# A gated cross-attention and mixture-of-experts kernel: the last pair of token tiles routed in another order

## The chip, the cores and the metric

The kernel runs on one NeuronCore of a Trainium2 chip. The core has five engines that run their own instruction streams and wait for one another through semaphores: TensorE (PE, matmuls; PEld is its weight load), VectorE (DVE), ScalarE (ACT), GpSimd (POOL) and SyncE (SP). Data moves between the chip's main memory and the on-chip memory through DMA queues, which SyncE, ScalarE and GpSimd issue to. The metric is the device time in microseconds (us) of one execution. A profile is one recorded execution; its times count from the span's start.

## The reference

The inputs are x (8 batches of 256 tokens, width 512), a context of 256 rows of 512 for each batch with a mask, two gates, a router (8 experts) and the experts' weights (512 to 192 and back). What is computed:

```
x = x + tanh(g_xattn) * attention(layernorm(x), ctx, ctx, mask)       # softmax over the unmasked rows, scale 1/sqrt(512)
xt = layernorm(x)                                                     # 2048 tokens
probs = softmax(xt @ w_router.T);  top_v, top_i = top_k(probs, 2);  top_v = top_v / sum(top_v)
for each token, over its two experts e:
    out += top_v * (silu(xt @ w_gate[e].T) * (xt @ w_up[e].T)) @ w_down[e].T
x = x + tanh(g_ffn) * out
```

Everything is float32. Which rows are masked and which experts a token takes depend on the data.

## The kernel before, in words

The 2048 tokens are 16 tiles of 128 tokens (NT = 16), in 8 pairs k of two tiles. There are two stages, and both are written out by hand in the order in which each engine is to take its work (`manual_schedule`).

**The routing stage** runs over steps s = 0 to 19 (line 579). Tile s gets its attention scores (`a_scores`), tile s - 1 its probabilities, its values and its router logits (`a_probs`, `a_values`), and tile s - 2 the centring of its updated row (`f_centre`) and a sum of squares (`f_square`). `a_values` (376) takes the two largest logits of each token (`max`, `max_index`, lines 386 and 387) and then adds the attention to x (line 388, the token update). Per pair, some steps later:

- `f_mark` (420): a one-hot mark of the expert of each choice, 128 x 32.
- `f_rank` (428): matmuls with a triangular matrix add the marks of this pair to a running count (`rank`), which gives each token its place in its expert's list; the place is split into a tile (`high`) and a row (`low`). `at_row` (line 441, VectorE) and `at_col` (line 445, four comparisons of 128 x 128 on GpSimd) are one-hot forms of the two.
- `f_table` (448): four matmuls of these add the token numbers to `table`, the list of tokens by place.
- `f_count` (455): two more matmuls bring the count up to date.
- `f_scale` (402): the variance and the difference of the two best logits on VectorE (lines 404, 406), then a power of -0.5 on GpSimd (407).
- `f_weigh` (410): weights from these on ScalarE (414 to 417), and the store of the pair's 256 rows, each with its scalars, to `xc_d` in main memory (418), issued from ScalarE.

After the last marks, `numbers` (509) works out on VectorE how many tiles each expert's list fills and where they begin: `u`, `nti`, `end`, `begin`, then `sel` (528), which selects the 46 expert tiles (23 for the first choices, 23 for the second), and `past`, `pn`, `eqi`, `nt_i` (530 to 535), the expert of each tile and the number of tiles. `read_table` (537) copies the table (539), and two matmuls with `sel` and one VectorE operation give `ids` (543), the token numbers of every expert tile. `last_constants` (493) makes constants that `numbers` reads (`ltile`, `keep`, `rowe`, `qplace`), on GpSimd, at step 15.

In the steps around the change the order of the last pair (k = 7) is: step 16: update of tile 15, `f_scale(6)`, `f_mark(7)`, `f_table(6)`; step 17: `f_rank(7)`, `f_square(15)`, `f_weigh(6)`, `f_count(7)`, `numbers`; step 18: `f_scale(7)`, `f_table(7)`, `read_table`; step 19: `f_weigh(7)`. Every engine takes its part of this in this order[...].

**The expert stage** (`run`, 700) takes 19 expert tiles of the first choices and 19 of the second. For each, GpSimd gathers 128 rows of `xc_d` by `ids` (line 640, up to four tiles ahead, and seven gathers before the first result is scattered). TensorE transposes them (181), applies the expert's gate and up weights (`gate_up`, 658) and its down weights (`down`, 682); GpSimd scatters the result (645), for the second choices after adding the first ones' result. The first gather needs `ids` and all eight row stores to have landed. The expert weights were loaded during the routing stage.

Of the kernel before, what the change touches and what calls it, by code (L numbers as in the profile page):

```python
# [9 lines left out]
FP = mybir.dt.float32  # L10
# [3 lines left out]
ALU = mybir.AluOpType  # L14
# [5 lines left out]
P = 128  # L20
# [26 lines left out]
def gated_xattn_moe(ctx: ExitStack, tc: tile.TileContext, x, xT, ctxn, ctxT, mask, maskT, g_x, g_f, wr, wgu, wd, out):  # L47
# [23 lines left out]
    def row(shape, name):  # L71
        return make(wk, 512, "row", 7, shape, name)
# [303 lines left out]
    def a_values(i):  # L376
        p, k, t = i // TT // 2, i // 2, i % 2
        if t == 0:
            KEEP["xr", k] = xrs[k % 4]
        lg = KEEP["xr", k][:, t, LG:LG + E1]  # L380
        prT, r, pcw = KEEP.pop(("prT", i)), KEEP.pop(("r", i)), KEEP.pop(("ppt", i))[:, P:2 * P]
        nc.tensor.matmul(pcw, lhsT=prT, rhs=cws[p], start=True, stop=True, skip_group_check=True)
        pav = bank([P, D], f"pav_{i}")
        nc.tensor.matmul(pav, lhsT=prT, rhs=cns[p], start=True, stop=True)  # L384
        nc.vector.scalar_tensor_tensor(lg, pcw[:, 0:E1], r, KEEP.pop(("xw", i)), ALU.mult, ALU.add)
        nc.vector.max(mx[:, i, :], lg[:, 0:E])
        nc.vector.max_index(ix[:, i, :], mx[:, i, :], lg[:, 0:E])
        nc.vector.scalar_tensor_tensor(xs[i], pav, r, xs[i], ALU.mult, ALU.add)

    def f_centre(i):  # L390
# [29 lines left out]
    def f_mark(k):  # L420
        m = marks[k % 2][:, NL:3 * NL]
        nc.vector.tensor_tensor(m.rearrange("p (t k e) -> p t k e", t=2, k=2), ecol.unsqueeze(1).broadcast_to([P, 2, 2, E]),
                                ix[:, 2 * k:2 * k + 2, 0:2].unsqueeze(3).broadcast_to([P, 2, 2, E]), ALU.is_equal)
# [4 lines left out]
    def f_rank(k):  # L428
        more(k, below, NL)
        more(k, ones, 0)  # L430
        at = sm_.tile([P, 2 * NL], FP, tag="at", bufs=2, name=f"at_{k}")
        nc.vector.tensor_mul(at, marks[k % 2][:, NL:3 * NL], rank[:, 0:2 * NL])
        pos = sm_.tile([P, 4], I32, tag="pos", bufs=2, name=f"pos_{k}")
        with nc.allow_low_precision(reason="whole numbers under 2 ** 16"):
            nc.vector.tensor_reduce(pos, at.rearrange("p (n e) -> p n e", n=4), AX.X, ALU.add)
        high = sm_.tile([P, 4], I32, tag="high", bufs=2, name=f"high_{k}")
        nc.vector.tensor_scalar(high, pos, 7, None, ALU.arith_shift_right)
        low = sm_.tile([P, 4], FP, tag="low", bufs=2, name=f"low_{k}")
        nc.vector.scalar_tensor_tensor(low, high, -float(P), pos, ALU.mult, ALU.add)  # L439
        at_row, at_col = row([P, 4, P], f"ar_{k}"), row([P, 4, P], f"ac_{k}")  # L440
        nc.vector.tensor_tensor(at_row, cols.unsqueeze(1).broadcast_to([P, 4, P]), high.unsqueeze(2).broadcast_to([P, 4, P]),
                                ALU.is_equal)
        for n in range(4):
            i = 2 * k + n // 2
            nc.gpsimd.tensor_scalar(at_col[:, n, :], cols, low[:, n:n + 1], idt[:, i:i + 1], ALU.is_equal, ALU.mult)  # L445
        KEEP["at", k] = at_row, at_col

    def f_table(k):
# [44 lines left out]
    def last_constants():  # L493
        any_ = dict(allow_small_or_imprecise_dtypes=True)
        nc.gpsimd.iota(ltile, pattern=[[0, 2], [-LT, E]], base=0, channel_multiplier=0, **any_)
        nc.gpsimd.memset(keep, 1.0)
        nc.gpsimd.memset(keep[:, 1, 0:1], 0.0)
        nc.gpsimd.affine_select(out=rowe, in_=ones[:, 0:E], pattern=[[-LT, E]], compare_op=ALU.is_ge, fill=0.0,
                                base=0, channel_multiplier=1)
        nc.gpsimd.affine_select(out=rowe, in_=rowe, pattern=[[LT, E]], compare_op=ALU.is_gt, fill=0.0,  # L500
                                base=LT, channel_multiplier=-1)
        nc.gpsimd.iota(qplace, pattern=[[1, NQ]], base=0, channel_multiplier=-1, **any_)

    ids = rt.tile([P, NS], U32, name="ids")
    eqi = rt.tile([1, NS], I32, name="eqi")
    nt_i = rt.tile([1, 2], I32, name="nt_i")
    sel = rt.tile([P, 2, NQ], FP, name="sel")

    def numbers():

        u = rt.tile([P, 2, E], I32, name="u")
        uf, lf = u.rearrange("p k e -> p (k e)"), ltile.rearrange("p k e -> p (k e)")
        nc.vector.tensor_scalar(uf, rank[:, 0:NL], float(P - 1), None, ALU.add)
        nc.vector.tensor_scalar(uf, uf, 7, None, ALU.arith_shift_right)
        nti = rt.tile([P, 2, E], FP, name="nti")
        nf = nti.rearrange("p k e -> p (k e)")
        nc.vector.tensor_tensor(nf, uf, lf, ALU.add)
        end = rt.tile([P, 2, E], FP, name="end")
        nc.vector.tensor_tensor_scan(end.rearrange("p k e -> p (k e)"), keep.rearrange("p k e -> p (k e)"), nf, 0.0,
                                     ALU.mult, ALU.add)  # L520
        nc.vector.tensor_sub(nti, end, nti)
        nc.vector.tensor_add(nf, nf, lf)
        for k in range(2):
            b = rt.tile([P, E], FP, name=f"rowb_{k}")
            begin = rt.tile([P, 1], FP, name=f"begin_{k}")
            nc.vector.tensor_mul(b, nti[:, k, :], rowe)
            nc.vector.tensor_reduce(begin, b, AX.X, ALU.add)
            nc.vector.tensor_scalar(sel[:, k, :], qplace, begin, None, ALU.is_equal)
        past = row([P, NS * E], "past")[0:1].rearrange("o (k q e) -> o k q e", k=2, q=NQ)
        nc.vector.tensor_tensor(past, end[0:1].unsqueeze(2).broadcast_to([1, 2, NQ, E]),  # L530
                                cols[0:1, 0:NQ].unsqueeze(1).unsqueeze(3).broadcast_to([1, 2, NQ, E]), ALU.is_le)
        pn = rt.tile([1, NS], FP, name="pn")
        nc.vector.tensor_reduce(pn, past.rearrange("o k q e -> o (k q) e"), AX.X, ALU.add)
        nc.vector.tensor_scalar(eqi, pn, float(E - 1), None, ALU.min)
        nc.vector.tensor_copy(nt_i, end[0:1, :, E - 1])

    def read_table():
        tb = row([P, 2, P], "tb")
        nc.scalar.copy(tb, table)
        pid = bank([P, NS], "pid")  # L540
        for k in range(2):
            nc.tensor.matmul(pid[:, k * NQ:(k + 1) * NQ], lhsT=tb[:, k, :], rhs=sel[:, k, :], start=True, stop=True)
        nc.vector.tensor_scalar(ids, pid, float(T), None, ALU.add)

    def on(f, i, n=NT):
        if 0 <= i < n:
            f(i)

    with tc.manual_schedule(engines={PE, DVE, ACT, POOL, SP}):
# [26 lines left out]
        m_centre(0)  # L576
        m_turn(0)
        m_gates()
        for s in range(NT + 4):
            odd = s % 2  # L580
            p, part = divmod(s, 4)
            on(a_probs, s - 1)
            on(f_centre, s - 2)
            if s:
                on(a_stats, s + 3)
                if not odd:
                    on(a_scale, (s + 2) // 2, NT // 2)
            on(a_scores, s)
            if s == 0:
                m_route(0)  # L590
                for n in range(1, NP):
                    m_pick(n)
                    m_fetch(n)
                a_stats(2)
                a_stats(3)
                a_scale(1)
                for b in range(1, B):
                    m_hide(b)
                more_constants()
            if odd:  # L600
                on(f_rank, (s - 3) // 2, NT // 2)
            on(a_values, s - 1)
            on(f_square, s - 2)
            if odd:
                on(f_weigh, (s - 5) // 2, NT // 2)
                on(f_count, (s - 3) // 2, NT // 2)
            else:
                on(f_scale, (s - 4) // 2, NT // 2)
                on(f_mark, (s - 2) // 2, NT // 2)
                on(f_table, (s - 4) // 2, NT // 2)  # L610
            if s == NT - 1:
                last_constants()
            if s == NT + 1:
                numbers()
            if s == NT + 2:
                read_table()
            if part == 2 and p + 1 < NP:
                m_mean(p + 1)
                m_centre(p + 1)
            if part == 3 and p + 1 < NP:  # L620
                m_turn(p + 1)
            if part == 0 and 0 < p < NP:
                m_route(p)
            if not odd and 3 <= (s + 4) // 2 < B:
                load_batch((s + 4) // 2)
            if 2 <= s < 2 + 2 * E:
                load_half(s - 2)
# [148 lines left out]
```

## Time and profile before

| | us |
|---|---|
| median of 3 runs (lowest, highest) | 320.92 (320.69, 323.11) |
| the profiled execution: its own time | 320.94 |
| the profiled execution: its span | 319.2 |
| TensorE busy in the span | 261.9 (82%) |
| GpSimd busy | 150.8 (47%) |
| VectorE busy | 131.7 (41%) |
| ScalarE busy | 115.4 (36%) |

In the profile's lines, a group or a piece of the timeline names its engine, its line in the code, the operation, what it writes and reads ("out<-in"), shapes and the number of instructions. In square brackets stands how long the engine was idle before it and what ended that. The busy time by stretch has the stretch, its length, the busy time (and count) of PE, PEld, DVE, ACT and POOL, the granted clock of TensorE as a share of full speed, the DMA engines' busy share and GB/s. A line of the waits has who waited, for whom, the total, the number of times and the longest. ACTq, POOLq and so on are an engine's instruction queue, which issues DMAs.

### The profile page before, as it was taken

To read this page: it belongs to the slowest core of one execution; us is meant where nothing else is said; L and a number is where in the kernel's file an instruction comes from. 1 tells how busy PE (TensorE), PEld (TensorE's weight loads), DVE (VectorE), ACT (ScalarE), POOL (GpSimd) and SP (SyncE) were. 2 spreads that over 40 slices of the span, in tenths; PEclk is the share of its full clock that TensorE was granted. 3 is DMA by queue.
4 is the path that set the end of the run, shared out by engine and by line. 5 is a ranking of instruction groups with operands and counts; after the bars stand their busy time and mean duration, and the time that the engine had idled before them with its cause. 6 is when DMAs were issued, how large, how long until landed. Compare 5 with 4: busy or idle time off the path is not lost. (4 is left out here: it accounts for less than half of the span.)

```text
span 319.2 us, 4026 instructions
## 1 busy us (share of the span) xinstructions
PE 261.9 (82%) x1100; PEld 165.7 (52%) x1100; DVE 131.7 (41%) x449; ACT 115.4 (36%) x275; POOL 150.8 (47%) x238
## 2 busy tenths in 40 slices
PE   3377897979850999999999999989999999999100
PEld 3265676767630566555555565545556555555000
DVE  3329988886760024333443334422242332425100
ACT  1123677767640233333332333323233332422100
POOL 4328855665654404253353443524656566444610
PEclk9999999999975699999999999999999999999855
DMA  5699769697214602233323324316355554423510
GB/s 165 222 349 310 249 231 341 221 367 280 94 75 130 203 3 90 88 106 105 113 93 109 103 99 137 105 57 177 129 150 160 166 173 148 139 76 100 161 61 0
DMA packets 16077, 48.55 MB, mean 152 GB/s; under 512 B 3181, under 2 KB 3181, under 8 KB 16048
## 3 DMA queue, kind: packets, MB, share of 16 engines
q0 software_dynamic: 7984, 25.64, 25.7%
q1 hardware_dynamic: 5888, 17.85, 16.3%
q10 hardware_dynamic: 2176, 4.72, 3.8%
q8 instruction: 13, 0.21, 0.3%
q14 instruction: 16, 0.13, 0.1%
HBM read 35.08 MB, written 14.68 MB: 156 GB/s over the span
## 5 line engine op out<-in xcount | busy, mean ns | idle before, releaser
L658 PE MATMUL pgu<-wgu_sb,xT_g 128*128 x304 | 106.1, 492 | 0.9 <-ACTq L728 0.9
L658 PEld LDWEIGHTS pgu<-wgu_sb,xT_g 128*128 128x128 f32 x304 | 58.1, 192 | 49.4 <-issue 17.9
L682 PE MATMUL py<-wd_sb,hT 96*128 x152 | 71.4, 592 | 0.0
L664 DVE SCALAR_TENSOR_TENSOR th<-th,pgu 128x192 f32<-128x192 f32 x38 | 13.5, 354 | 103.0 <-ACT th L663 103.0
L645 POOL DMA_INDIRECT acc_d<-y,ids x19 | 19.3, 1015 | 60.3 <-DVE y L688 57.6
L640 POOL DMA_INDIRECT xall<-xc_d,ids x38 | 37.0, 975 | 17.9 <-DMA xc_d<-xr 5.0
L663 ACT ACTIVATE th<-pgu,xall 128x192 f32<-128x192 f32 x38 | 16.0, 421 | 75.2 <-PE pgu L658 75.2
L686 ACT ACTIVATE y<-py,xall 128x512 f32<-128x512 f32 x38 | 26.1, 687 | 42.1 <-PE py L682 40.0
L682 PEld LDWEIGHTS py<-wd_sb,hT 96*128 96x128 f32 x152 | 25.9, 190 | 18.8 <-issue 18.8
L445 POOL TENSOR_SCALAR ac<-cols,low,idt 128x128 f32<-128x128 f32 x32 | 27.5, 869 | 14.8 <-DVE low L439 13.8
L645 POOL DMA_INDIRECT out<-y,ids x19 | 19.3, 1015 | 31.6 <-DVE y L695 29.3
L181 PE MATMUL pt_g<-ident,xall 128*128 128x128 f32 x152 | 23.8, 281 | 8.8 <-issue 8.3
L183 ACT COPY xT_g<-pt_g 128x512 f32<-128x512 f32 x38 | 22.3, 586 | 19.6 <-PE pt_g L181 19.6
L688 DVE SCALAR_TENSOR_TENSOR y<-xall,y 128x512 f32<-128x512 f32 x19 | 14.3, 752 | 28.7 <-ACT y L686 28.7
L181 PEld LDWEIGHTS pt_g<-ident,xall 128*128 128x128 f32 x152 | 18.3, 144 | 9.6 <-issue 8.5
L354 PE MATMUL psc<-cT,xT 128*128 128x137 f32 x128 | 19.1, 293 | 3.9 <-ACT cT L268 3.2
L640 POOL DMA_INDIRECT acc<-acc_d,ids x19 | 18.2, 957 | 5.4 <-issue 5.4
L354 PEld LDWEIGHTS psc<-cT,xT 128*128 128x128 f32 x128 | 17.0, 199 | 5.0 <-ACT cT L268 3.9
L384 PE MATMUL pav<-cn,prT 128*128 128x512 f32 x32 | 16.4, 594 | 0.0
L695 DVE TENSOR_TENSOR y<-y,acc 128x512 f32<-128x512 f32 x19 | 12.9, 680 | 8.4 <-DMA acc<-acc_d,ids 8.2
L666 DVE SCALAR_TENSOR_TENSOR h<-th,xall,pgu 128x192 f32<-128x192 f32 x38 | 15.8, 415 | 1.4
L673 PEld LDWEIGHTS pht<-ident,h 128*96 128x96 f32 x76 | 9.6, 126 | 12.7 <-issue 7.5
(149 smaller groups left out, 294.7 us busy)
## 6 DMA issues: line engine op xcount, KB each, us to landing
wgu_sb<-wgu SPq DMA_DIRECT2D x8, 768.0 KB, 7.9
xc_d<-xr ACTq DMA_DIRECT2D x8, 576.0 KB, 4.0
xT<-xT SPq DMA_DIRECT2D x8, 512.0 KB, 5.0
wd_sb<-wd SPq DMA_DIRECT2D x8, 384.0 KB, 7.1
xall<-x SPq DMA_DIRECT2D x1, 2048.0 KB, 13.3
xall<-x SPq DMA_DIRECT2D x2, 512.0 KB, 4.1
xall<-x SPq DMA_DIRECT2D x1, 1024.0 KB, 9.2
xall<-xc_d,ids POOLq DMA_INDIRECT x38, 3.5
```

The lines of the kernel that those rows point to most:

```text
L181: nc.tensor.transpose(pt[:, c, :], src[:, c * P:(c + 1) * P], ident)
L183: nc.scalar.copy(dst, pt)
L354: nc.tensor.matmul(both, lhsT=xTs[b][:, c, t * P:(t + 1) * P], rhs=cTs[p % 2][:, c, :], start=(c == 0), stop=(c == HC - 1))
L384: nc.tensor.matmul(pav, lhsT=prT, rhs=cns[p], start=True, stop=True)
L445: nc.gpsimd.tensor_scalar(at_col[:, n, :], cols, low[:, n:n + 1], idt[:, i:i + 1], ALU.is_equal, ALU.mult)
L640: nc.gpsimd.indirect_dma_start(out=g, out_offset=None, in_=src[:, :], in_offset=bass.IndirectOffsetOnAxis(ap=ids[:, q:q + 1], axis=0))
L645: free(nc.gpsimd.indirect_dma_start(out=dst, out_offset=bass.IndirectOffsetOnAxis(ap=ids[:, q:q + 1], axis=0), in_=z, in_offset=None, boun ...
L658: nc.tensor.matmul(pgu, lhsT=xgT[:, c, :], rhs=wgu_sb[:, bass.ds(v * GU + c * 2 * I, 2 * I)], start=(c == 0), stop=(c == HC - 1))
L663: nc.scalar.activation(th, pgu[:, 0:I], AF.Tanh, scale=xg[:, RS:RS + 1])
L666: nc.vector.scalar_tensor_tensor(h, th, xg[:, R2:R2 + 1], pgu[:, I:2 * I], ALU.mult, ALU.mult)
L682: nc.tensor.matmul(py, lhsT=hT[:, k, :], rhs=wd_sb[:, bass.ds(v * DN + k * D, D)], start=(k == 0), stop=(k == 1))
L686: nc.scalar.activation(y, py, AF.Copy, scale=xg[:, c:c + 1])
```

## The change

Five edits, the first four on the last pair:

1. `f_mark(7)` stands ahead of the token update of tile 15 instead of behind it.
2. `f_scale(7)` stands inside `f_rank(7)`, behind `low` and ahead of the one-hot forms, instead of behind `numbers`. With it its power on GpSimd stands ahead of the comparisons.
3. `f_weigh(7)`, with the store of the last rows, stands ahead of `f_table(7)` and `read_table`, instead of behind them.
4. Of the four comparisons of `at_col`, VectorE takes the first two and GpSimd the last two.
5. `numbers` is shorter: the row of the table at which each expert's tiles begin is added into `qplace` beforehand (`place`, `first`, `place_rows`, at steps 12 and 14), so that one sum and one multiplication and reduction fall away; its last part becomes `experts`, which stands behind `ids`. `last_constants` moves from step 15 to step 12. `f_square` stands ahead of `f_rank` in a step.

```diff
--- before.py
+++ after.py
@@ -385,6 +385,8 @@
         nc.vector.scalar_tensor_tensor(lg, pcw[:, 0:E1], r, KEEP.pop(("xw", i)), ALU.mult, ALU.add)
         nc.vector.max(mx[:, i, :], lg[:, 0:E])
         nc.vector.max_index(ix[:, i, :], mx[:, i, :], lg[:, 0:E])
+        if i == NT - 1:
+            f_mark(k)
         nc.vector.scalar_tensor_tensor(xs[i], pav, r, xs[i], ALU.mult, ALU.add)
 
     def f_centre(i):
@@ -437,12 +439,16 @@
         nc.vector.tensor_scalar(high, pos, 7, None, ALU.arith_shift_right)
         low = sm_.tile([P, 4], FP, tag="low", bufs=2, name=f"low_{k}")
         nc.vector.scalar_tensor_tensor(low, high, -float(P), pos, ALU.mult, ALU.add)
+        last = k == NT // 2 - 1
+        if last:
+            f_scale(k)
         at_row, at_col = row([P, 4, P], f"ar_{k}"), row([P, 4, P], f"ac_{k}")
         nc.vector.tensor_tensor(at_row, cols.unsqueeze(1).broadcast_to([P, 4, P]), high.unsqueeze(2).broadcast_to([P, 4, P]),
                                 ALU.is_equal)
         for n in range(4):
             i = 2 * k + n // 2
-            nc.gpsimd.tensor_scalar(at_col[:, n, :], cols, low[:, n:n + 1], idt[:, i:i + 1], ALU.is_equal, ALU.mult)
+            by = nc.vector if last and n < 2 else nc.gpsimd
+            by.tensor_scalar(at_col[:, n, :], cols, low[:, n:n + 1], idt[:, i:i + 1], ALU.is_equal, ALU.mult)
         KEEP["at", k] = at_row, at_col
 
     def f_table(k):
@@ -500,11 +506,22 @@
         nc.gpsimd.affine_select(out=rowe, in_=rowe, pattern=[[LT, E]], compare_op=ALU.is_gt, fill=0.0,
                                 base=LT, channel_multiplier=-1)
         nc.gpsimd.iota(qplace, pattern=[[1, NQ]], base=0, channel_multiplier=-1, **any_)
+        place = rt.tile([P, E], FP, name="place")
+        nc.gpsimd.iota(place, pattern=[[LT, E]], base=0, channel_multiplier=0, **any_)
+        nc.gpsimd.tensor_tensor(place, place, rowe, ALU.mult)
+        KEEP["place"] = place
+
+    def place_rows():
+        first = rt.tile([P, 1], FP, name="first")
+        nc.vector.tensor_reduce(first, KEEP.pop("place"), AX.X, ALU.add)
+        nc.vector.tensor_scalar(qplace, qplace, first, None, ALU.add)
 
     ids = rt.tile([P, NS], U32, name="ids")
     eqi = rt.tile([1, NS], I32, name="eqi")
     nt_i = rt.tile([1, 2], I32, name="nt_i")
     sel = rt.tile([P, 2, NQ], FP, name="sel")
+
+    end = rt.tile([P, 2, E], FP, name="end")
 
     def numbers():
 
@@ -515,17 +532,16 @@
         nti = rt.tile([P, 2, E], FP, name="nti")
         nf = nti.rearrange("p k e -> p (k e)")
         nc.vector.tensor_tensor(nf, uf, lf, ALU.add)
-        end = rt.tile([P, 2, E], FP, name="end")
         nc.vector.tensor_tensor_scan(end.rearrange("p k e -> p (k e)"), keep.rearrange("p k e -> p (k e)"), nf, 0.0,
                                      ALU.mult, ALU.add)
         nc.vector.tensor_sub(nti, end, nti)
-        nc.vector.tensor_add(nf, nf, lf)
+        nc.vector.tensor_mul(nti, nti, rowe.unsqueeze(1).broadcast_to([P, 2, E]))
+        begin = rt.tile([P, 2], FP, name="begin")
+        nc.vector.tensor_reduce(begin, nti, AX.X, ALU.add)
         for k in range(2):
-            b = rt.tile([P, E], FP, name=f"rowb_{k}")
-            begin = rt.tile([P, 1], FP, name=f"begin_{k}")
-            nc.vector.tensor_mul(b, nti[:, k, :], rowe)
-            nc.vector.tensor_reduce(begin, b, AX.X, ALU.add)
-            nc.vector.tensor_scalar(sel[:, k, :], qplace, begin, None, ALU.is_equal)
+            nc.vector.tensor_scalar(sel[:, k, :], qplace, begin[:, k:k + 1], None, ALU.is_equal)
+
+    def experts():
         past = row([P, NS * E], "past")[0:1].rearrange("o (k q e) -> o k q e", k=2, q=NQ)
         nc.vector.tensor_tensor(past, end[0:1].unsqueeze(2).broadcast_to([1, 2, NQ, E]),
                                 cols[0:1, 0:NQ].unsqueeze(1).unsqueeze(3).broadcast_to([1, 2, NQ, E]), ALU.is_le)
@@ -576,7 +592,7 @@
         m_centre(0)
         m_turn(0)
         m_gates()
-        for s in range(NT + 4):
+        for s in range(NT + 2):
             odd = s % 2
             p, part = divmod(s, 4)
             on(a_probs, s - 1)
@@ -597,23 +613,27 @@
                 for b in range(1, B):
                     m_hide(b)
                 more_constants()
+            on(f_square, s - 2)
             if odd:
                 on(f_rank, (s - 3) // 2, NT // 2)
             on(a_values, s - 1)
-            on(f_square, s - 2)
             if odd:
-                on(f_weigh, (s - 5) // 2, NT // 2)
                 on(f_count, (s - 3) // 2, NT // 2)
+                on(f_weigh, (s - 5) // 2, NT // 2 - 1)
             else:
-                on(f_scale, (s - 4) // 2, NT // 2)
-                on(f_mark, (s - 2) // 2, NT // 2)
-                on(f_table, (s - 4) // 2, NT // 2)
-            if s == NT - 1:
+                on(f_scale, (s - 4) // 2, NT // 2 - 1)
+                on(f_mark, (s - 2) // 2, NT // 2 - 1)
+                on(f_table, (s - 4) // 2, NT // 2 - 1)
+            if s == NT - 4:
                 last_constants()
+            if s == NT - 2:
+                place_rows()
             if s == NT + 1:
                 numbers()
-            if s == NT + 2:
+                f_weigh(NT // 2 - 1)
+                f_table(NT // 2 - 1)
                 read_table()
+                experts()
             if part == 2 and p + 1 < NP:
                 m_mean(p + 1)
                 m_centre(p + 1)
```

## The prediction

> **What bounds the kernel now.** I read the page's slices first, then the busy time by stretch, then the timeline of the two ends of the hole these show, then the waits in that place.
>
> The slices (part 2 of the page, 7.98 us each):
>
> ```profile
> PE   3377897979850999999999999989999999999100
> PEclk9999999999975699999999999999999999999855
> ```
>
> Slice 12 (95.8 to 103.7 us) has a TensorE that does nothing, and slices 11 to 13 a lower clock. On both sides TensorE is busy. After the hole it is the bound: in the busy time by stretch (TensorE first, clock and DMA last)
>
> ```profile
> 110.00:160.00 50.00, 50.00 (x186) 29.32 (x185) 18.42 (x41) 17.27 (x31) 16.42 (x24) 1.00 0.26 83
> 210.00:260.00 50.00, 50.00 (x183) 28.91 (x182) 15.77 (x38) 16.95 (x30) 27.67 (x36) 1.00 0.47 144
> ```
>
> it has no idle time, a tile every 4.95 us. So what moves the first expert tile moves the end by as much, except for the clock. The chain that ended last names GpSimd in this part, but with TensorE full that is only the other side of the same period.
>
> What holds the first tile, from the timeline (start, length, engine, line, operation):
>
> ```profile
> 89.00 0.68 DVE L441 TENSOR_TENSOR ar<-cols,high 128x512 f32<-128x512 f32 x1
> 89.27 3.47 POOL L445 TENSOR_SCALAR ac<-cols,low,idt 128x128 f32<-128x128 f32 x4 [0.99 <-PE rank L426]
> 89.77 0.37 ACTq L418 DMA_DIRECT2D xc_d<-xr  x1
> 93.62 0.37 ACT L539 COPY tb<-table 128x256 f32<-128x256 f32 x1 [3.88 <-PE table L452]
> 93.68 0.15 DVE L404 TENSOR_SCALAR ve<-ve 128x2 f32<-128x2 f32 x1
> 93.91 0.72 POOL L407 TENSOR_TENSOR xr<-ve,expo 128x2 f32<-128x2 f32 x1 [1.18 <-DVE d L406]
> 95.13 0.21 DVE L543 TENSOR_SCALAR ids<-pid 128x46 uint32<-128x46 f32 x1 [1.24 <-PE pid L542]
> 95.88 0.37 ACTq L418 DMA_DIRECT2D xc_d<-xr  x1
> 99.63 1.15 POOL L640 DMA_INDIRECT xall<-xc_d,ids  x1 [5.00 <-DMA xc_d<-xr]
> ...
> 105.86 4.45 PE L658 MATMUL pgu<-wgu_sb,xT_g 128*128 x8
> ```
>
> Two chains meet at the first gather (99.63). Row numbers `ids` are there at 95.34. The last row store leaves only at 95.88 and lands for the gather 3.75 us later. GpSimd sits idle 5.0 us for it:
>
> ```profile
> POOL xall L640 <- DMA xc_d<-xr: 5.0, 1, 5.0
> PE pt_g L181 <- issue: 8.3, 1, 8.3
> ```
>
> The store is late because VectorE prepares its scalars (L404) only at 93.68, behind the whole numbering, although the square that L404 reads was complete at 88.67 (accumulator read, 88.48 plus 0.19). The first eight gate_up matmuls then take 4.45 us at half clock, against 2.75 in later tiles.
>
> [...]the store's bytes move from 96.6 to 98.4, the gather starts at 99.63. [...]comparisons of L445 take 0.788 us, but the one that starts beside `ar` (L441) takes 1.102, ending 0.69 after `ar`. [...]The trace has 0.55 in 92 to 93 us, 0.50 until 109, and 0.92 in 109 to 110, 5.7 us after TensorE began again.
>
> **The change part by part,** in the times of the profiled run.
>
> *Marks ahead of the update* (second tile of the last pair). FIND_INDEX8 ends at 86.25. The mark can start at 86.3 instead of 87.21, the update L388 some 0.1 later than its 86.41. The rank matmuls, now at 87.45 after 0.19 of waiting for the mark, can't pass the table matmuls ahead of them, which end at 87.26: gain 0.19. `at` 88.20 becomes 88.01, `low` 88.92 becomes 88.73. On ScalarE everything after the update is 0.1 later: the accumulator is read by 88.77, and pair 6's row store (89.77) leaves at 89.87.
>
> *Scalars ahead of the numbering.* `ve` now stands behind `low` and waits for ScalarE's 88.77: a new wait, with `ar`, the comparisons, the numbering and `ids` queued behind it. `low` ends at 88.89, so it costs nothing to 0.1. `ve` 88.9, `d` 88.97. GpSimd's power (L407) started 0.23 after `ve`: 89.13, now ahead of the comparisons. [...]blocked by `ar` alone at about 90.35; with the two comparisons on VectorE passing it too, 90.7. I take 90.35, as the 1.102 row shows blocking.
>
> *Row store ahead of the table copy.* ScalarE issues pair 6's store until 90.27 (0.40 from issue to the next operation, as in 84.29 to 84.70). From the power's end to the last store's issue was 94.63 to 95.88, 1.25. So the issue is at 90.35 + 1.25 = 91.6 (ends 91.5 and 91.95). Pair 6's bytes moved from 90.6 to 92.3; the last store's started 0.7 after its issue, so at 92.3: they just miss each other[...]. The gather can start at 91.6 + 3.75 = 95.35 (95.2 to 95.9).
>
> *Comparisons shared.* GpSimd loses two of four (2 x 0.79). VectorE gains two. No row shows this operation there: [...]`sel` (128x23, 0.33, L528) one from above. I take 0.25: the numbering starts at 89.72 + 0.5 = 90.2 instead of 89.61[...]. GpSimd's two then run from 90.45 to 92.05, against an end at 92.74. The last comparison to `tb` took 0.88: `tb` at 92.9.
>
> *Numbering shortened.* From `u` to the end of `sel` took 89.61 to 92.49, 2.88. Gone are L522 (0.28 to the next start) and one multiply and reduction (91.81 to 92.25, 0.44): 2.16, so `sel` is done at 92.4, ahead of `tb`[...]. `tb` to the end of `ids` was 1.72: `ids` at 94.65, usable at 94.85, which leaves 0.5 of slack to the store's 95.35.[...]
>
> *What is moved elsewhere.* The constants (86.63 to 87.58, 0.95) go to step 12 with an iota (0.15) and a multiply (0.24 as the nearest small row, 0.72 as the power): 1.3 to 1.8 us, in GpSimd's wait of 2.6 before 76.11. Without this cover, 1.8. Two small VectorE operations (0.16 and 0.33) go to step 14, in its idle 0.88 before 81.81; uncovered 0.5. The power of pair 6 loses the constants ahead of it, worth nothing, since ScalarE is at the square until 88.67. The expert numbers (`past` to `nt_i`, 92.39 to 93.76, 1.4) go behind `ids`, done by 96.1; TensorE needs them at its first gate_up, some 101.6: hidden by 5 us, else 1.4. Nothing moves on SyncE.
>
> *Sum.* Gather 99.63 to 95.35: 4.3 us. TensorE's hole begins at about 94.4 instead of 95.1 and ends at 99.1 instead of 103.37: 4.7 long[...]. Gate_up paid 4.45 - 2.75 = 1.7 for that. [...]of which I take a little, 0.1. Span 319.2 - 4.4 = 314.8; with the 1.74 around it (320.94 - 319.2) 316.5, and I say 316.6. The profiled time is 0.02 above the median of 320.92, so nothing is corrected.
>
> **The rivals.** [...](0.16): power, comparisons and numbering take turns on VectorE and GpSimd, and `ids` or the store come 0.6 to 1.5 later. For it speaks that VectorE's new work lies beside GpSimd's; against it that only one row of before shows more than 0.3. Time 317.2 to 318.2. *The clock does better* (0.10): the shorter hole doesn't cool TensorE, [...]another 1.3: 315.2. Against it: 0.55 already at 92 to 93, in sparse work before the hole. *The transfer is hidden anyway* (0.04): the two stores run into each other and the second lands nearly as before; 576 KB take 1.8, a gain of 1 to 2 is left, 319 to 320. *Slower* (0.04): TensorE stays at half clock for longer after the earlier start, while its first tiles arrive at the rate of the gathers. [...]Against it: before, the clock returned after 5.7 us with the same work.
>
> **How the numbers follow.** My case (0.66) is 316.6, itself 315.8 to 317.3. The range leaves out the slower case, the hidden transfer, half of the better clock[...], 0.16 in all: 315.2 to 318.2. About 1% is what a measurement can tell: faster means under 317.7. My case nearly whole, the clock[...] give 0.82; the rest of these and the hidden transfer 0.14; slower 0.04.
>
> **What would show it.** Right: the last row store issued between 91.4 and 92, the first gather at 95.2 to 95.9, GpSimd's wait ahead of it on the store and only about 3 us, TensorE's hole 4 to 5 us, and the same 4.95 per tile. The power should last over 1 us beside `ar`. Wrong: a first gather released by `ids`, a table copy later than 93.3, a second gate_up at half clock, or a routing stage that is already later at 80 us.

## The result, and the profile after

The changed kernel takes 317.38 us (median of 4 runs, 316.94 to 317.68), the kernel before 321.29 (4 runs, 320.69 to 323.11). The ratio is 0.9868, its 95% interval 0.9824 to 0.9911: 1.3% faster. Forecast were 316.6 and a range of 315.2 to 318.2. The profiled execution of the changed kernel took 317.67, its span 315.8.

In the page's slices (now 7.9 us each) the hole of TensorE is still there, shorter, and the granted clock is low around it as before, down to five tenths:

```profile
PE   3377797979863999999999999999999999999100
PEclk9999999999985799999999999999999999999855
```

In these two stretches behind the hole TensorE has no idle time, as before (between them it waits once, 0.94 us before and 0.85 now):

```profile
110.00:160.00 50.00, 50.00 (x187) 29.30 (x186) 18.86 (x42) 17.27 (x31) 18.47 (x27) 1.00 0.27 86
210.00:260.00 50.00, 50.00 (x183) 28.89 (x182) 16.21 (x40) 16.95 (x30) 28.76 (x37) 1.00 0.51 153
```

The timeline from the last update to the first expert tile (lines are some 2 to 20 higher than in the kernel before):

```profile
86.74 0.19 DVE L424 TENSOR_TENSOR mark<-ecol,ix 128x32 f32<-128x32 f32 x1
...
87.53 0.16 DVE L406 TENSOR_SCALAR ve<-ve 128x2 f32<-128x2 f32 x1
...
89.15 0.17 DVE L406 TENSOR_SCALAR ve<-ve 128x2 f32<-128x2 f32 x1
89.30 0.69 DVE L446 TENSOR_TENSOR ar<-cols,high 128x512 f32<-128x512 f32 x1
89.40 1.14 POOL L409 TENSOR_TENSOR xr<-ve,expo 128x2 f32<-128x2 f32 x1 [0.85 <-DVE d L408]
89.90 0.60 DVE L451 TENSOR_SCALAR ac<-cols,low,idt 128x128 f32<-128x128 f32 x2
90.22 0.37 ACTq L420 DMA_DIRECT2D xc_d<-xr  x1
90.53 1.59 POOL L451 TENSOR_SCALAR ac<-cols,low,idt 128x128 f32<-128x128 f32 x2
91.90 0.37 ACTq L420 DMA_DIRECT2D xc_d<-xr  x1
92.70 0.37 ACT L555 COPY tb<-table 128x256 f32<-128x256 f32 x1 [0.82 <-PE table L458]
94.21 0.21 DVE L559 TENSOR_SCALAR ids<-pid 128x46 uint32<-128x46 f32 x1 [1.79 <-PE pid L558]
95.67 1.15 POOL L660 DMA_INDIRECT xall<-xc_d,ids  x1 [3.55 <-DVE eqi L550]
...
101.97 5.12 PE L678 MATMUL pgu<-wgu_sb,xT_g 128*128 x8
```

The last store leaves at 91.90 instead of 95.88, the first gather starts at 95.67 instead of 99.63, and the first eight gate_up matmuls take 5.12 us instead of 4.45. The name in the gather's brackets (`eqi`) is not a producer of anything that the gather reads; it only ended last in this profile. What really ended last has to be shown by experiment.

The two profiles don't start alike: everything in the routing stage is 0.45 us later in the second one from about 21 us on, before any edit (the last section comes to that). It is not the edits' doing: two versions below that keep all but one of them reach the same place at 86.95 and 87.07. So I measure from a fixed point just ahead of the edits, the start of pair 6's scalars on VectorE (L404, now L406): 87.08 before, 87.53 now. From there the first gather starts 12.55 us later before, 8.14 now. The difference of the spans, 319.2 - 315.8 = 3.4, is the sum of

| stretch | us |
|---|---|
| up to pair 6's scalars (87.08, 87.53) | +0.45 |
| from there to the first gather (12.55, 8.14) | -4.41 |
| from it to the first gate_up (6.23, 6.30) | +0.07 |
| from there to the next tile's transposes (4.29, 4.96) | +0.67 |
| the rest, to the end (209.05, 208.87) | -0.18 |

### The profile page after: what moved, and what is told of

The parts are those of the page before. It is cut to its first block, busy times and chain, and to the rows that moved or that the text cites. A ratio compares the mean times of both kernels' runs of the same rounds, so it can differ in the third digit from the quotient of the medians.

```text
span 315.8 us, 4021 instructions
## 1 busy us (share of the span) xinstructions
PE 261.9 (83%) x1100; PEld 165.9 (53%) x1100; DVE 132.1 (42%) x450; ACT 115.4 (37%) x275; POOL 149.8 (47%) x238
## 5 line engine op out<-in xcount | busy, mean ns | idle before, releaser
L451 POOL TENSOR_SCALAR ac<-cols,low,idt 128x128 f32<-128x128 f32 x30 | 25.7, 869 | 12.4 <-DVE low L441 12.4
```

The costliest lines, as they stand in the source:

```text
L451: by.tensor_scalar(at_col[:, n, :], cols, low[:, n:n + 1], idt[:, i:i + 1], ALU.is_equal, ALU.mult)
```

## The experiments

The theory is that of the prediction: the first gather is released by the last row store, the store's gain is the change's gain, and the other edits only keep the token numbers from becoming the later of the two. Each set of versions ran beside runs of the kernel before (medians of 321.46, 321.61 and 321.39), and the ratios are to those. "Gather at" means from here on: us from the start of pair 6's scalars to the first gather.

**The last store taken away.** This version leaves out the last pair's own rows; pair 5's stand in their place, stored together with pair 5's own store:

```diff
-        nc.scalar.dma_start(out=xc_d[2 * k * P:2 * (k + 1) * P, :]..., in_=xr)
+        for j in {NT // 2 - 1: [], NT // 2 - 3: [k, NT // 2 - 1]}.get(k, [k]):
+            nc.scalar.dma_start(out=xc_d[2 * j * P:2 * (j + 1) * P, :]..., in_=xr)
```

> The changed kernel, but the rows of the last pair are stored with those of pair 5 (that pair's rows, so the last pair's own rows never reach main memory), and nothing is stored behind the last scalars. Theory (the last row store releases the first gather): the gather waits for the token numbers instead, complete at 94.4 in the changed kernel's profile, so it starts at 94.6 to 94.9 instead of 95.67, 0.8 to 1.1 us earlier: 316.3 to 316.6. Rival (the token numbers already release it): no change, 317.4.

Measured: 317.21 (316.17 to 319.08, 4 runs; ratio to before 0.9869, 0.9801 to 0.9936), and gather at 7.18 instead of 8.14. The timeline now names the token numbers, and the gather follows 0.29 us behind their end:

```profile
94.74 0.21 DVE L560 TENSOR_SCALAR ids<-pid 128x46 uint32<-128x46 f32 x1 [1.79 <-PE pid L559]
95.24 1.17 POOL L661 DMA_INDIRECT xall<-xc_d,ids  x1 [2.59 <-DVE ids L560]
```

So the store does hold the first gather in the changed kernel, by 0.96 us. The median is only 0.2 under the changed kernel's, within the spread of both; this verdict rests on the trace.

**The store late again,** the other three edits kept:

```diff
-        if last:
-            f_scale(k)
...
                 numbers()
-                f_weigh(NT // 2 - 1)
+                f_scale(NT // 2 - 1)
                 f_table(NT // 2 - 1)
                 read_table()
                 experts()
+                f_weigh(NT // 2 - 1)
```

> The changed kernel with the scalars of the last pair behind the numbering and its row store behind the table copy again; the other three edits stay. Theory (nearly all of the gain is the earlier store): numbering ends near 92.2 without the power ahead of it, power near 93.2, store issued near 94.4, gather at 98.2, 2.5 us later: 319.9. Rival (the shorter numbering and the shared comparisons carry the gain): 317.4 to 318.

Measured: 319.54 (15 runs; ratio 0.9939, 0.9918 to 0.9960). Gather at 10.31, 2.17 later than in the changed kernel; the trace names the store, 3.73 behind its issue:

```profile
94.53 0.21 DVE L557 TENSOR_SCALAR ids<-pid 128x46 uint32<-128x46 f32 x1 [0.78 <-PE pid L556]
95.74 0.37 ACTq L420 DMA_DIRECT2D xc_d<-xr  x1
99.47 1.15 POOL L659 DMA_INDIRECT xall<-xc_d,ids  x1 [4.98 <-DMA xc_d<-xr]
```

As the theory says. The remaining edits by themselves bring 12.55 to 10.31, 2.24: not by earlier numbers, but because less stands ahead of the scalars on VectorE. From the start of `u` to the scalars it took 4.07 us before and takes 1.78 here: the sums up to `sel` end some 1.0 sooner, and the expert numbers, 1.3, have gone behind `ids`.

**The store early, and no other edit** (on the kernel before; the square has to move ahead of the ranks with it, since the scalars read it):

```diff
+        if k == NT // 2 - 1:
+            f_scale(k)
         at_row, at_col = row([P, 4, P], f"ar_{k}"), row([P, 4, P], f"ac_{k}")
...
+            on(f_square, s - 2)
             if odd:
                 on(f_rank, (s - 3) // 2, NT // 2)
             on(a_values, s - 1)
-            on(f_square, s - 2)
...
                 numbers()
+                f_weigh(NT // 2 - 1)
```

> The kernel before with the last pair's scalars ahead of its comparisons and its row store ahead of the table copy, and nothing else of the change. Theory: store as in the changed kernel, but four comparisons on GpSimd behind the power end near 93.7 and the token numbers near 96.0 then hold the gather, 96.2: 3.4 us less than before, 317.9. Rival (the parts only work together: numbering behind the power takes its place): gather at 98 or later, 319.5.

Measured: 318.36 (317.91 to 319.69, 4 runs; ratio 0.9899, 0.9834 to 0.9963). Gather at 9.44, 3.11 earlier than before, 1.30 later than with the whole change. The four comparisons behind the power end at 93.9, the token numbers at 96.5, and these release the gather at 96.80:

```profile
90.66 3.23 POOL L447 TENSOR_SCALAR ac<-cols,low,idt 128x128 f32<-128x128 f32 x4
...
94.78 0.37 ACT L541 COPY tb<-table 128x256 f32<-128x256 f32 x1 [2.89 <-PE table L454]
96.30 0.21 DVE L545 TENSOR_SCALAR ids<-pid 128x46 uint32<-128x46 f32 x1 [2.23 <-PE pid L544]
96.80 1.15 POOL L643 DMA_INDIRECT xall<-xc_d,ids  x1 [2.90 <-DVE ids L545]
```

The mechanism is the expected one. The price of the missing edits is higher than the 0.5 expected. Counted from pair 6's scalars, the comparisons end 0.36 later than expected; the table copy comes 0.89 behind the last of them instead of 0.58 as in the changed kernel (TensorE's last four table matmuls take 1.64 here, in the changed kernel twice two take 0.49 each); and the gather comes 0.3, not 0.2, behind the numbers.

**Four comparisons on GpSimd,** the rest as changed:

```diff
-            by = nc.vector if last and n < 2 else nc.gpsimd
+            by = nc.gpsimd
```

> The changed kernel with all four comparisons of the last pair on GpSimd again. Theory (the shared comparisons keep the token numbers just ahead of the store): GpSimd ends 2 x 0.79 later, 93.7 instead of 92.1; the table copy and the token numbers follow by 1.6, numbers at 96.0, gather at 96.2 instead of 95.67: 317.9. Rival (sharing buys nothing[...]): the store, no longer behind two comparisons, is 0.1 earlier: 317.3.

Measured: 318.97 (12 runs; ratio 0.9897, 0.9870 to 0.9925). Gather at 9.02, 0.88 later (0.5 was expected; the table copy comes 0.88 behind the last comparison here too), released by the numbers:

```profile
91.10 1.13 POOL L409 TENSOR_TENSOR xr<-ve,expo 128x2 f32<-128x2 f32 x1 [0.85 <-DVE d L408]
...
92.23 3.12 POOL L451 TENSOR_SCALAR ac<-cols,low,idt 128x128 f32<-128x128 f32 x4
...
96.23 0.37 ACT L555 COPY tb<-table 128x256 f32<-128x256 f32 x1 [2.66 <-PE table L458]
97.75 0.21 DVE L559 TENSOR_SCALAR ids<-pid 128x46 uint32<-128x46 f32 x1 [4.12 <-PE pid L558]
98.25 1.17 POOL L660 DMA_INDIRECT xall<-xc_d,ids  x1 [2.90 <-DVE ids L559]
```

The profiled run is 1.7 us late from the routing stage, so its absolute times aren't to be compared, and its own time of 319.87 is the highest of the twelve (lowest 317.35). Sharing the comparisons is what keeps the numbers ahead of the store.

**The longer numbering again,** and **the marks behind the update again:**

```diff
-        nc.vector.tensor_mul(nti, nti, rowe.unsqueeze(1).broadcast_to([P, 2, E]))
-        begin = rt.tile([P, 2], FP, name="begin")
-        nc.vector.tensor_reduce(begin, nti, AX.X, ALU.add)
+        nc.vector.tensor_add(nf, nf, lf)
         for k in range(2):
-            nc.vector.tensor_scalar(sel[:, k, :], qplace, begin[:, k:k + 1], None, ALU.is_equal)
+            b = rt.tile([P, E], FP, name=f"rowb_{k}")
+            begin = rt.tile([P, 1], FP, name=f"begin_{k}")
+            nc.vector.tensor_mul(b, nti[:, k, :], rowe)
+            nc.vector.tensor_reduce(begin, b, AX.X, ALU.add)
+            nc.vector.tensor_scalar(sel[:, k, :], qplace, begin, None, ALU.is_equal)
...
-            if s == NT - 2:
-                place_rows()
```

> The changed kernel with the longer numbering again (the addition, and a multiplication and a reduction for each half), 0.7 us on VectorE. Theory (the store holds the gather; the numbering ends 0.3 ahead of the table copy): token numbers 0.1 to 0.4 later, gather as before: 317.4 to 318.1 as in the two looks at the changed kernel. Rival (the numbering is what lets the gather start): gather 0.7 later.

```diff
-        if i == NT - 1:
-            f_mark(k)
         nc.vector.scalar_tensor_tensor(xs[i], pav, r, xs[i], ALU.mult, ALU.add)
...
-                on(f_mark, (s - 2) // 2, NT // 2 - 1)
+                on(f_mark, (s - 2) // 2, NT // 2)
```

> The changed kernel with the last marks behind the token update again. Theory: the rank matmuls stand behind the table matmuls in any case, the row store hangs on the square, which is 0.1 earlier now: gather within 0.1 of 8.1 us behind pair 6's scalars, no difference in time. Rival (the mark is at the head of everything): gather 0.2 or more later.

Longer numbering: 316.69 (316.09 to 319.01, 4 runs), gather at 8.14, exactly as with the whole change:

```profile
91.45 0.37 ACTq L420 DMA_DIRECT2D xc_d<-xr  x1
...
95.21 1.15 POOL L660 DMA_INDIRECT xall<-xc_d,ids  x1 [3.54 <-DVE eqi L552]
```

`sel` ends 0.60 later (at 5.48 instead of 4.88), still 0.1 ahead of the matmuls that read it. Beside the other edits the saved sums are worth nothing; the expert numbers stay behind `ids` in this version. Marks behind: 318.04 (316.55 to 319.30, 8 runs), gather at 8.32, the store 0.18 later (4.55 instead of 4.37):

```profile
91.50 0.37 ACTq L418 DMA_DIRECT2D xc_d<-xr  x1
...
95.27 1.15 POOL L658 DMA_INDIRECT xall<-xc_d,ids  x1 [3.44 <-DVE past L544]
```

In time neither can be told from the changed kernel. In the trace the mark is worth 0.18 us, which is against the expectation: the step on VectorE behind the rank matmuls (`at`) comes at 0.67 instead of 1.13, and as the scalars now stand behind it, the store gains too. It gains less than `at` does, because in the changed kernel the scalars have only the square left to wait for, which is read by 1.59 with the mark early and by 1.60 without.

**TensorE kept busy in its hole.** The measure beside it is a second set of runs of the changed kernel:

> The changed kernel once more, as the measure beside the others of this set. All theories: 317.4, first gather 8.1 us after pair 6's scalars on VectorE begin, as in its first profile; the first eight gate_up matmuls between 3.9 and 5.1 us.

Measured: 318.14 (317.12 to 319.23, 4 runs; ratio 0.9880, 0.9836 to 0.9924), gather at 8.15, gate_up 5.29, a little over what was expected:

```profile
102.01 5.29 PE L678 MATMUL pgu<-wgu_sb,xT_g 128*128 x8
```

Then the changed kernel with added matmuls whose results nobody reads (each is two records in the trace, so that 16 of them show as x32):

```diff
+    def fill(n, new=False):
+        if new:
+            KEEP["fill"] = bank([P, P], "fill")
+        for _ in range(n):
+            nc.tensor.matmul(KEEP["fill"], lhsT=ones, rhs=wgu_sb[:, 0:P], start=True, stop=True, ...)
...
+                fill(4, True)
                 numbers()
...
                 read_table()
+                fill(16)
```

> The changed kernel with 20 matmuls of 128x128 into an unused bank, 4 between the last count and the table matmuls and 16 behind the token numbers, in TensorE's hole. Theory (the hole costs a half clock, which is worth 5.12 - 2.75 = 2.4 us in the first gate_up, and two transposes of 0.5 more): the first gate_up takes near 2.75, 2.0 to 2.4 us less: 315.0 to 315.4. Rival ([...]the added matmuls push the transposes): 317.4 to 318.

Measured: 315.13 (314.90 to 317.08, 4 runs; ratio 0.9801, 0.9755 to 0.9847), 3.0 under the changed kernel beside it. The gather is where it was (8.14); gate_up takes 2.82 instead of 5.29, and the next tile's transposes come 2.59 earlier (17.00 against 19.59). In the timeline of TensorE the added matmuls leave 2.05 us idle, and the granted clock reads 1.00 from 88 to 106 us:

```profile
93.58 3.82 PE L565 MATMUL fill<-wgu_sb,ones 128*128 128x128 f32 x32
99.45 0.63 PE L181 MATMUL pt_g<-ident,xall 128*128 128x128 f32 x4 [2.05 <-DMA xall<-xc_d,ids]
...
101.86 2.82 PE L686 MATMUL pgu<-wgu_sb,xT_g 128*128 x8 [0.20 <-DMA xall<-xc_d,ids]
```

It is not the hole alone that the added matmuls fill. Without them the clock falls ahead of the hole, where TensorE still works, but thinly. In the kernel before the hole begins at 95.1, in the changed one at 94.2, and the granted clock (third number from the end) is down by then, at 0.55 and 0.50 in the kernel before and at 0.50 from 93 us on in the changed one; the first two lines are of the kernel before, the last two of the changed one:

```profile
92.00:93.00 1.00, 0.96 (x3) 0.67 (x4) 0.88 (x4) 0.00 (x0) 0.73 (x1) 0.55 0.22 77
93.00:94.00 1.00, 0.58 (x2) 0.28 (x2) 0.86 (x5) 0.37 (x1) 0.09 (x1) 0.50 0.00 0
92.00:93.00 1.00, 0.49 (x2) 0.30 (x2) 0.38 (x2) 0.30 (x1) 0.12 (x1) 0.98 0.84 313
93.00:94.00 1.00, 0.88 (x4) 0.88 (x4) 0.00 (x0) 0.07 (x1) 0.00 (x0) 0.50 0.99 392
```

In the kernel before, TensorE was busy for 0.16, 0.49 and 0.49 of the three microseconds from 89 to 92, and no pause in the five ahead of the fall is longer than 1.26 us. Which of the 20 matmuls are needed, the 4 ahead of the hole or the 16 in it, was not tried.

The same on the kernel before, with 4 and 24 matmuls:

> The kernel before with 28 matmuls of 128x128 into an unused bank, 4 behind the last count and 24 behind the token numbers, in its longer hole. Theory (the half clock is a cost of the hole, apart from the change): the first gate_up falls from 4.45 to near 2.8, 1.7 to 2.2 us less, 319.3 to 319.8, and the filled changed kernel (315.1) stays about 4.4 ahead, which is what the earlier gather alone is worth. Rival (TensorE's hole is shorter in the changed kernel, and part of its gain is a better clock): less than 1 us, 320.5 or more.

Measured: 320.59 (20 runs; ratio 0.9972, 0.9951 to 0.9993). This failed as an experiment: the matmuls were over too early, 3.55 us ahead of the transposes, and TensorE was slow again (the transposes 1.08, gate_up 4.40, in its timeline):

```profile
93.84 5.60 PE L549 MATMUL fill<-wgu_sb,ones 128*128 128x128 f32 x48
102.99 1.08 PE L181 MATMUL pt_g<-ident,xall 128*128 128x128 f32 x4 [3.55 <-DMA xall<-xc_d,ids]
```

So it doesn't decide how the kernels compare in a filled hole. The median 0.8 under that of the kernel before is not explained by the gate_up, which is only 0.05 shorter. The version shows two other things. Behind the added matmuls the transposes took 0.63 after 2.05 us of idling in the filled changed kernel, and 1.08 after 3.55 here. And in the kernel before, token numbers that come 0.73 earlier (7.32 instead of 8.05) leave the gather at 12.55:

```profile
94.03 0.21 DVE L543 TENSOR_SCALAR ids<-pid 128x46 uint32<-128x46 f32 x1 [0.51 <-PE pid L542]
95.51 0.37 ACTq L418 DMA_DIRECT2D xc_d<-xr  x1
99.26 1.15 POOL L648 DMA_INDIRECT xall<-xc_d,ids  x1 [4.99 <-DMA xc_d<-xr]
```

Before, too, it was the store.

**The store split.** The 512 values of the last rows go from SyncE as soon as they are centred; only the 64 scalars wait for the weights:

```diff
+    def store_values(k):
+        nc.sync.dma_start(out=xc_d[2 * k * P:2 * (k + 1) * P, 0:D]..., in_=xrs[k % 4][:, :, 0:D])
...
+        lo = D if k == NT // 2 - 1 else 0
-        nc.scalar.dma_start(out=xc_d[2 * k * P:2 * (k + 1) * P, :]..., in_=xr)
+        nc.scalar.dma_start(out=xc_d[2 * k * P:2 * (k + 1) * P, lo:XW]..., in_=xr[:, :, lo:XW])
...
+            if s == NT + 1:
+                store_values(NT // 2 - 1)
```

> The changed kernel, but the 512 values of the last pair's rows are stored from SyncE as soon as they are centred, and only their 64 scalars behind the last weights, from ScalarE. Theory (the landing of 576 KB, not its issue alone, holds the gather): the 64 KB land before the token numbers, the gather is released by these, 0.8 to 1.0 us earlier as without the last store: 316.4. Rival (the landing is a fixed time, or 256 rows of 256 bytes are as slow): 317.4.

> The split store and the 20 added matmuls together. Theory: both, 314.2 to 314.6. Rival: one takes the place of the other, 315.0 or more.

Measured: split 316.70 (315.64 to 318.78, 4 runs; ratio 0.9842, 0.9787 to 0.9896), gather at 7.41, 0.74 earlier:

```profile
91.56 0.37 ACTq L425 DMA_DIRECT2D xc_d<-xr  x1
...
93.86 0.21 DVE L564 TENSOR_SCALAR ids<-pid 128x46 uint32<-128x46 f32 x1 [1.80 <-PE pid L563]
94.59 1.15 POOL L667 DMA_INDIRECT xall<-xc_d,ids  x1 [2.81 <-DVE past L551]
```

The small store takes 3.03 from issue to gather, against 3.77. The numbers end 0.52 ahead of the gather, and a gather that they released came 0.29 behind them, so it is still the store, by some 0.2, against the expectation. Both together: 314.12 (313.59 to 314.96, 4 runs; ratio to before 0.9760, 0.9724 to 0.9797), gather at 7.03, gate_up 2.82; the small store takes 2.65 here, and why it is quicker stays open. The two gains (1.4 and 3.0 alone, 4.0 together) nearly add up. This is the fastest version, 4.0 under the changed kernel beside it.

**TensorE kept busy at the start too,** with nine more matmuls ahead of the first context transposes (all the added ones multiply the identity matrix here, not the weights):

```diff
+        fill(9, True)
         m_turn(0)
```

> The split store and the 20 added matmuls, and 9 more of 128x128 in TensorE's idle stretch at 10 to 15 us, ahead of the first context transposes. Theory (TensorE is at half speed from there until 20 to 28 us, the eight score matmuls taking 2.16 against 1.10 later, and when that ends differs by run): those take near 1.1 and the router matmuls near 1.06 instead of 1.9, the last pairs come 1.5 to 2.2 earlier: 312.0 to 312.7. Rival (that stretch waits for the loads anyway[...]): under 0.5 us.

Measured: 314.87 (313.96 to 315.99, 4 runs): no gain. The score matmuls do take 1.18 instead of 2.16. But the added ones begin only at 13.2 us, not at 10.4, where TensorE's work before them ends, so they push the transposes from 15.0 to 17.2, more than the faster matmuls win back, and pair 6's scalars come at 87.71 (87.04 without). Whether a better place would help stays open. This trace also shows how little the length of a pause says: the sixteen in the hole take 5.44 us here, against 3.82 in the version without the nine, in spite of the four matmuls ahead of the hole and with no pause of TensorE over 0.5 us in the four us before. The transposes behind them take 0.60 and 0.66, gate_up 2.82.

## Why the prediction was right

The case called likeliest happened, by its own steps, though not quite at its own time. It was given 315.8 to 317.3; the medians are 317.38 and, in the second set, 318.14, which is where the first rival stood (turns on VectorE and GpSimd, 317.2 to 318.2). Its mechanism is not what happened: the power took 1.14 us in the changed kernel and 1.13 and 1.14 in the two versions in which VectorE makes no comparisons, and 0.72 with the store late, where it doesn't run beside `ar`; so the longer power goes with `ar` alone, and numbers and store came earlier than forecast, not later. Against the kernel before beside it the gain is 3.9 us in the first set and 3.5 in the second, with 4.3 to 4.4 forecast. Numbers of the changed kernel's profile are given less 0.45 here, so that they stand in the time of the profile before.

- *What bounds it:* right. TensorE is full behind the hole but for one wait, and the row store holds the gather before and after: the runs without the last store and with it late show the second, the numbers that came earlier for nothing in the kernel before the first.
- *Marks:* forecast were 0.19 for `at`, and the update, the square and pair 6's store 0.1 later. `at` came 0.45 earlier (87.75): the rank matmuls began at 87.10, ahead of the modelled end of the table matmuls (87.26) that was to hold them. The price did not come: the square was read by 88.67 and pair 6's store left at 89.77, both as before. Hence `low` was done 0.26 earlier than forecast, and the mark is worth 0.18 at the last store.
- *Scalars:* `ve` forecast at 88.9, was 88.70; the power forecast to be held up by `ar` and to end at 90.35, lasted 1.14 instead of 0.72 and ended at 90.09. To price it by the one comparison that took 1.102 beside `ar`, where the others took 0.788, was right.
- *Store:* issue forecast 91.6, was 91.45 (1.36 behind the power, forecast 1.25); landing 3.75, was 3.77; gather 95.35, was 95.22.
- *Comparisons and numbering:* the two comparisons on VectorE took 0.60, forecast 0.5; that is 0.30 for one, near the estimate of 0.25. The numbering took 1.99, forecast 2.16. The table copy came at 92.25 (forecast 92.9): GpSimd was done at 91.67 instead of 92.05, and TensorE's granted clock was still 0.98 in 92 to 93 us of its own profile (0.55 in the profile before); its last two table matmuls took 0.49, and the copy came 0.58 behind the last comparison, not 0.88. The end of the numbers was 93.97 (94.65). The slack to the store was 0.96, forecast 0.5. The prediction had that these edits count only as cover for the store, but not which of them gives the cover: sharing the comparisons is worth 0.88 of gather time beside the others, the mark 0.18, the shorter sums nothing.
- *Moved work:* hidden as forecast. The constants with the two new operations lie at 73.5 to 74.7, in GpSimd's wait before 76.11.
- *The sum:* the gather gained 4.41 from the fixed point, forecast 4.3. What is missing between 316.6 and the 317.67 of the profile is the clock and the start. The clock was forecast 0.1 better, an estimate with no measurement under it, and the stretch behind it was 0.67 worse: the first gate_up took 5.12, 2.4 more than in later tiles (2.75). And the 0.45 of the routing stage was not in the sum at all: I took the stage ahead of the edits as the same in each execution.
- *The signs:* TensorE's hole was to be 4 to 5 us and was 5.27, since the numbers were done earlier and the gather was not. A routing stage that is later at 80 us was named as a sign of being wrong, and it was later, by 0.45; it says nothing against the mechanism, as it starts ahead of the edits.

So the mechanism was right, and that the time stayed inside the range is in part luck: the range had room for a worse clock only because it was wide. What the first gate_up takes was not understood. In the four profiles of the changed kernel and of versions with the gather at 8.1 to 8.3 and no added matmuls it is 4.85 to 5.29, in the kernel before 4.45, so the extra seems to go with the change. It does not go with the length of the hole: 8.78 us of hole had 4.13, 4.42 had 3.86 and 4.46 had 5.38. And the prediction put the half clock down to the hole, while in the kernel before the clock read 0.55 and 0.50 in 92 to 94 us, ahead of the hole at 95.1, in thin work.

## What to carry over

Where two chains meet at one wait, price both to the end, and ask of each edit which of the two it shortens: here one part moved the store by four microseconds, and another was worth its 0.9 only because it kept the other chain ahead of it. A transfer that must land can be cut into what is ready early and what is not (here 3.03 us from issue to gather instead of 3.77). And the hole of TensorE with the thin work ahead of it had two prices here, its own length and a granted clock of 0.50 behind it; added matmuls ahead of the hole and in it, which ended 2.05 and 0.95 us ahead of the real work, took away the second (gate_up 2.82 in both, against 5.29).

## What was not expected

Far into the routing stage TensorE's matmuls take up to twice as long as later (eight score matmuls 2.16 us at 17 us, 1.10 later), and for how long differs by execution. In the profile with four comparisons on GpSimd, the third set of index matmuls at 24 us and the score matmuls after it are still slow (TensorE's timeline):

```profile
24.21 1.22 PE L219 MATMUL pidx<-mval,oh 128*128 128x128 f32 x4 [0.58 <-DVE oh L215]
...
25.44 2.03 PE L354 MATMUL psc<-cT,xT 128*128 128x137 f32 x8
```

while in that of the split store with added matmuls they are fast:

```profile
22.98 0.71 PE L219 MATMUL pidx<-mval,oh 128*128 128x128 f32 x4 [0.58 <-DVE oh L215]
...
23.64 1.10 PE L354 MATMUL psc<-cT,xT 128*128 128x137 f32 x8
```

The first set of index matmuls, at 20 us, takes 1.06 in the slow one of these two, 0.63 in the fast one, 0.61 in the kernel before and 0.91 in the changed kernel's first profile. There this and the matmuls just ahead of it (1.92 against 1.77 before) make most of the 0.45 us. Pair 6's scalars come at 89.2 in the two profiles that stay slow past 24 us and at 86.7 to 88.1 in the others: over 2 us of a kernel's time, as much as most of the edits are worth, and from a stretch that lies ahead of all of them. The granted clock of the records reads 1.00 from 8 to 34 us in the profiles of the two kernels and of the versions with four comparisons on GpSimd, with the store late and with the split store and added matmuls; only the lengths of the matmuls show it. What decides when they get short was not settled.
